# A message-passing layer on one core: SyncE fetches the rows of every 68th quad instead of every 48th, one batch in two steps instead of three in four

## The chip, the cores and the metric

The kernel runs on one core of one Trainium2 chip. The metric is device time in microseconds (us) of one launch. A core has five engines that run their own instruction streams: TensorE (PE, matrix multiply; PEld is its weight load), VectorE (DVE), ScalarE (ACT), GpSimd (POOL) and SyncE (SP, which here only issues DMA transfers). They meet through semaphores. 16 DMA engines move the data.

## What is computed

One equivariant graph layer over N = 12,500 nodes (160 features: 64 scalars and 32 vectors of 3) and E = 400,000 edges, sorted by destination, followed by a residual sum and a layer norm:

```python
h_s = s @ lin1_ws * a / 8                          # node features, 64 wide
h_v = einsum('nci,cd->ndi', v, lin1_wv) * a / sqrt(32)
hid = silu(edge_scalars @ fc_w1 / 8)               # per edge, 64 wide
w1, w2, w3, w4, w5 = split(hid @ fc_w2 / 8, ...)   # per edge, 224 wide
es, ev = h_s[edge_src], h_v[edge_src]              # gather of 160 floats per edge
m_s1 = w1 * es * e0;   m_s2 = w4 * (ev . e1) / sqrt(3)
m_v1 = (w2 * es) x e1; m_v2 = w3 * ev * e0; m_v3 = w5 * cross(ev, e1) / sqrt(2)
agg  = segment_sum(concat(...), edge_dst) / 4
o    = agg @ lin2;     pre = s @ sc + o
out  = layernorm(x + [silu(pre_s[:64]), sigmoid(pre_s[64:]) * pre_v])
```

The line that matters here is the gather: for each of 400,000 edges, one row of 160 floats (640 bytes) is read from a table that the kernel has written to HBM.

## The kernel before

**Start.** The first 61 us compute `h` for all nodes and write it to the table `h_tab` in HBM (L235 to L364). Constants and weights are loaded and scaled.

**Tiles, quads, steps.** The edges make 3,125 tiles of 128. Four tiles are a *quad* (`Q = 4`), and the main loop (L900) does one quad in a step: 782 steps. Six steps are a *chunk* of 24 tiles (`CT`).

**One step n, by engine.** The program is in the order in which it is written (`manual_schedule`, L891); nothing moves instructions afterwards.
- SP: `fetch(n + 4)` (L904). Where step n + 4 begins a chunk, it issues the load of that chunk's edge scalars, `es`, two transfers of 384 KB (L206). This load waits for the weights matmul of the step before (`mark`, L207), so SP can't run a chunk ahead. Now and then it also loads indices (L156), edge attributes (L157), and pieces for other work (L646, L692, L779, L781).
- SP: `fetch_rows(n)` (L905), which the change touches; see below.
- POOL: `gather` (L906, L473): four indirect DMAs, one for each tile, fetch 128 rows of `h_tab` each into `hg`. There are four `hg` buffers (the pool `deep`), so POOL can be four quads ahead of VectorE.
- PE: `weights` (L515), two matmuls for the 224 weights of each edge, from `hid`.
- ACT: copies out of PSUM and the silu (L460, L606, L608, L819), held back until the weights matmul of the step.
- DVE: `one_hot` (L578), `products` of weights and gathered rows (L525, L533), `select_quad` (L587), and additions into the accumulator (L631).
- PE: `add_tile` (L594) for the quad of two steps ago: a matmul with the one-hot rows sums the messages by destination.
- PE: `hide(n + 3)` (L939, L456), every second step, the hidden layer of two later steps. It reads `es`: this is where PE needs SP's load.
- PE and ACT now and then: transposes (L603), the second linear map (L623), and the end of finished nodes (L656 to L692).

**SyncE's own quads.** The step numbers in `own` (L478) are quads that POOL does not gather; SP fetches their rows one at a time. Before, `OWN = 48` gives 56, 104, ..., 776: 16 quads. For such a quad m:
- at step m - 54, `places` (L482) loads its 512 indices into `at_bytes`, four small transfers (L488);
- at step m - 46, DVE multiplies them by the 640 bytes of a row (L756), and `rows_of` (L491) makes 32 *jobs*;
- a job (L496) loads 16 indices into SP's registers (`BATCH = 16`, L497, a TENSOR_LOAD) and issues 16 transfers of 640 bytes, one for each row (L502; each is a register MOVE and a DMA);
- L759 says in which steps one job is issued: `n % EVERY and rows_due` with `EVERY = 4`, so in three steps of every four, 48 rows in four steps. The 32 jobs of quad m go out in steps m - 46 to m - 5;
- one `hq` buffer takes the rows (L493). Step m uses it in place of `hg` (L906).

What sets SP's order is thus written out by hand: a job stands in SP's queue ahead of the next step's `es` load.

Of the kernel before, what the change touches and what calls it, by code (L numbers as in the profile page):

```python
# [35 lines left out]
CT = 2 * SIDE  # L36
AHEAD = 3 * CT
NF = 4
OWN = 48
BATCH = 16  # L40
EVERY = 4

MARGIN = 128
NO = 16
# [13 lines left out]
def gnn_kernel(  # L58
# [176 lines left out]
    with tc.tile_pool(name="nodes", bufs=len(starts)) as nodes, tc.tile_pool(  # L235
# [84 lines left out]
        for c0, cn, quarters, cq, xa, xz in loaded:  # L320
# [6 lines left out]
            for t0 in range(0, nt, U):  # L327
                ps = nps.tile([P, U, P], F32, name="hp")
                for t in range(t0, min(t0 + U, nt)):
                    n = min(P, cn - t * P)  # L330
# [6 lines left out]
                if t0 + k < nt <= t0 + U:  # L337
                    n = cn - full * P
# [6 lines left out]
            for u in range(-(-cq // P)):  # L345
                n = min(P, cq - u * P)
# [10 lines left out]
            if cn > full * P:  # L357
                n = cn - full * P
# [118 lines left out]

    own = [n for n in range(OWN + 8, len(steps) - 4, OWN) if len(steps[n][2]) == Q]  # L478
    by_bytes = h_tab.rearrange("n d -> (n d)").bitcast(U8)
    row_bytes = 4 * D  # L480

    def places(pool, n):  # L482

        at_bytes = pool.tile([Q, P], I32, name="at_bytes")
        for k, (t, _, _) in enumerate(steps[n][2]):
            g, u = divmod(t, GT)
            with nc.allow_non_contiguous_dma(reason="the indices of one tile"):
                nc.sync.dma_start(at_bytes[k:k + 1], src[g][:, u:u + 1].rearrange("p u -> u p"))  # L488
        return at_bytes

    def rows_of(pool, at_bytes):  # L491

        hq = pool.tile([P, Q, D], F32, name="hq", bufs=1)  # L493
        flat_hq = hq.rearrange("p t d -> p (t d)").bitcast(U8)

        def job(t, p0):  # L496
            _, values = nc.values_load_multi_w_load_instructions(  # L497
                at_bytes[t:t + 1, p0:p0 + BATCH], engines=[ENG.SP], min_val=0,
                max_val=(N - 1) * row_bytes,
                skip_runtime_bounds_check_because="every entry of src is the index of a node")  # L500
            for p, v in enumerate(values, p0):
                nc.sync.dma_start(flat_hq[p:p + 1, t * row_bytes:(t + 1) * row_bytes],  # L502
                                  by_bytes[ds(v, row_bytes)][None])

        return hq, [lambda t=t, p0=p0: job(t, p0) for t in range(Q) for p0 in range(0, P, BATCH)]
# [198 lines left out]
    with tc.tile_pool(  # L704
# [43 lines left out]
        at_of, hq_of, rows_due = {}, {}, []  # L748

        def fetch_rows(n):  # L750

            for m in own:
                if n == max(1, m - OWN - 6):
                    at_of[m] = places(mine, m)
                if n == m - OWN + 2:
                    nc.vector.tensor_scalar_mul(at_of[m], at_of[m], float(row_bytes))  # L756
                    hq_of[m], jobs = rows_of(mine, at_of[m])
                    rows_due.extend((m, job) for job in jobs)
            if n % EVERY and rows_due:  # L759
                rows_due.pop(0)[1]()  # L760
            assert all(m > n for m, _ in rows_due)

# [128 lines left out]
        with tc.manual_schedule(engines={ENG.PE, ENG.DVE, ENG.Activation, ENG.Pool, ENG.SP}):  # L891
# [8 lines left out]
            for n, (c, i, tiles) in enumerate(steps):  # L900
                if 2 <= n < 2 + ZP // 2:
                    for k in range(2):
                        clear(2 * (n - 2) + k)
                fetch(n + 4)  # L904
                fetch_rows(n)  # L905
                hg = hq_of.pop(n) if n in own else gather(deep, [index(t) for t, _, _ in tiles])  # L906
                pw, marks[0] = weights(pw_ps, hids[c, i // 2], [(half, u - i // 2 * 4) for _, half, u in tiles])
# [39 lines left out]
            n = len(steps)  # L947
# [141 lines left out]
```

## Time and profile before

| | before |
|---|---|
| median of 3 runs | 6075.9 us (6064.73 to 6079.05) |
| the profiled execution, its own time | 6075.9 us |
| its span, first to last instruction | 6074.1 us |
| mean granted TensorE clock | 0.822 of full speed |
| PE busy / DVE / ACT / POOL | 4037.2 / 2446.3 / 853.9 / 2915.8 us |
| gathers by POOL (L473) | 3061, 948 ns mean each |
| rows by SP (L502) | 8192, in 512 jobs |
| HBM | 67 GB/s over the span |

How to read it. SP does no arithmetic: its instructions are sequencer instructions, which the profile does not count as busy, so SP has no share in the table of engines and has to be read from its own timeline and waits. In a timeline row the columns are the start, the length, the engine (`SPq` is SP's sequencer), the line, the operation, output and input, the number of instructions merged into the row, and in brackets the idle time before it and what ended it. A row of waits has the engine and line that waited, what it waited for, the total in us, the number of times, and the longest. "remote" is a semaphore whose sender the profile does not name. A row of a table by windows has the window, its length, and then busy us and instruction count of PE, PEld, DVE, ACT and POOL, the granted clock, the DMA engines' busy share and GB/s.

### The profile page before, as it was taken

The numbers are of one execution on the slowest core, as the hardware profiler recorded it, in microseconds if no ns is written. First come the engines' busy times: TensorE is split into PE (matmuls) and PEld (weight loads), VectorE is DVE, ScalarE is ACT, GpSimd is POOL, SyncE is SP. The second block draws the span as 40 slices with busy tenths as digits, with TensorE's granted clock in tenths as the row PEclk, the third lists the DMA queues.
The fourth block names the chain that finished last, engine by engine and source line by source line (L and its number), as shares of the span: only waits on it lengthen the run. The fifth ranks groups of instructions, "written<-read, shape, count | busy, mean of one in ns | idle before, by whom it ended". The sixth has DMA issues, their size and how long they took to land. (4 is left out here: it accounts for less than half of the span.)

```text
span 6074.1 us, 63034 instructions
## 1 busy us (share of the span) xinstructions
PE 4037.2 (66%) x14291; PEld 1740.4 (29%) x14291; DVE 2446.3 (40%) x6524; ACT 853.9 (14%) x2488; POOL 2915.8 (48%) x3080
## 2 busy tenths in 40 slices
PE   6667676676666666676767667667666666766666
PEld 3223222232322222232223223223222232322223
DVE  4434343343443433443434434344344343443434
ACT  2111111111111111111111111111111111111111
POOL 4444454444444444454545445445444444554443
PEclk8778788788888888788878788888788887888888
DMA  6223222222222222232222222223232222222222
GB/s 169 61 60 71 64 68 68 62 67 62 70 66 64 67 62 63 66 72 62 69 66 66 68 65 68 60 65 71 64 71 64 63 64 70 68 64 63 69 63 53
DMA packets 250347, 412.82 MB, mean 68 GB/s; under 512 B 88267, under 2 KB 180935, under 8 KB 249063
## 3 DMA queue, kind: packets, MB, share of 16 engines
q0 software_dynamic: 149200, 261.29, 18.0%
q1 hardware_dynamic: 100246, 147.32, 10.5%
q14 instruction: 273, 2.24, 0.1%
q8 instruction: 114, 1.87, 0.1%
q10 hardware_dynamic: 514, 0.10, 0.0%
HBM read 392.44 MB, written 16.00 MB: 67 GB/s over the span
## 5 line engine op out<-in xcount | busy, mean ns | idle before, releaser
L473 POOL DMA_INDIRECT hg<-h_tab,idx x3061 | 2901.5, 948 | 3072.2 <-DVE pr L533 1713.6
L515 PE MATMUL pw<-w,hid 128*128 128x448 f32 x3126 | 1544.4, 623 | 14.1 <-issue 9.1
L594 PE MATMUL pa<-pr,sel 128*64 128x416 f32 x6250 | 1339.0, 548 | 223.5 <-ACT sa L819 214.3
L578 DVE TENSOR_TENSOR pw<-rel,iota 128x64 f32<-128x64 int16 x782 | 181.8, 232 | 3195.3 <-PE pw L515 1424.6
L456 PE MATMUL misc<-es,w 128*128 128x512 f32 (+1 forms) x784 | 528.8, 763 | 944.2 <-DMA es<-in_es_t_dram 774.3
L533 DVE TENSOR_TENSOR pr<-pw,hg 128x384 f32<-128x384 f32 x2298 | 1128.5, 546 | 0.0
L515 PEld LDWEIGHTS pw<-w,hid 128*128 128x128 f32 x3126 | 671.6, 224 | 679.4 <-issue 653.3
L594 PEld LDWEIGHTS pa<-pr,sel 128*64 128x64 f32 x6250 | 393.9, 142 | 1167.4 <-issue 907.1
L606 ACT COPY tt<-misc 128x192 f32<-128x192 f32 x521 | 166.7, 320 | 3521.5 <-PE pw L515 1978.8
L603 PE MATMUL misc<-ident,sa 128*128 128x128 f32 x2084 | 387.1, 315 | 373.1 <-ACT tt L608 201.8
L525 DVE TENSOR_TENSOR pr<-pw,hg 128x512 f32<-128x512 f32 x766 | 528.9, 690 | 29.2 <-issue 1.6
L603 PEld LDWEIGHTS misc<-ident,sa 128*128 128x128 f32 x2084 | 255.0, 157 | 707.3 <-issue 364.8
L456 PEld LDWEIGHTS misc<-es,w 128*128 128x128 f32 x784 | 140.2, 224 | 1060.4 <-issue 981.6
L623 PE MATMUL misc<-tt,l 128*96 128x256 f32 (+5 forms) x1496 | 354.1, 385 | 1.7 <-ACT tt L608 1.5
L460 ACT ACTIVATE hid<-misc 128x512 f32<-128x512 f32 x392 | 238.4, 608 | 669.7 <-remote 397.6
L587 DVE TENSOR_TENSOR sel<-pw,eas 128x256 f32<-128x256 f32 x782 | 321.5, 411 | 0.3
L819 ACT COPY sa<-pa 128x416 f32<-128x416 f32 x521 | 267.9, 514 | 205.7 <-PE pw L515 123.4
L623 PEld LDWEIGHTS misc<-tt,l 128*96 128x96 f32 (+1 forms) x1496 | 226.5, 165 | 132.3 <-issue 57.1
L631 DVE TENSOR_TENSOR acc<-acc,os 96x32 f32 x1042 | 204.9, 197 | 25.1 <-ACT os L626 6.9
L785 PE MATMUL misc<-xs,scs 64*96 64x500 f32 x50 | 42.2, 939 | 234.9 <-DMA xs<-in_xs_t_dram 234.9
L656 PE MATMUL misc<-ident,acc 96*128 96x96 f32 x196 | 41.0, 297 | 200.9 <-DVE acc L631 166.0
L786 DVE TENSOR_TENSOR acc<-acc,misc 96x500 f32<-96x500 f32 x50 | 33.5, 670 | 261.3 <-PE misc L785 206.2
(87 smaller groups left out, 715.4 us busy)
## 6 DMA issues: line engine op xcount, KB each, us to landing
hq<-h_tab SPq DMA_DIRECT2D x8192, 0.6 KB
es<-in_es_t_dram SPq DMA_DIRECT2D x258, 384.0 KB
hg<-h_tab,idx POOLq DMA_INDIRECT x3061
h_tab<-ht POOLq DMA_DIRECT2D x6, 1280.0 KB
xt<-in_x_dram SPq DMA_DIRECT2D x23, 320.0 KB
out_dram<-y SPq DMA_DIRECT2D x23, 320.0 KB
xv<-in_xv_t_dram SPq DMA_DIRECT2D x25, 187.5 KB
xs<-in_xs_t_dram SPq DMA_DIRECT2D x25, 125.0 KB
```

The costliest lines, as they stand in the source:

```text
L456: nc.tensor.matmul(ph[:k, c], w1[:k, :k], es[:k, t0 * P + c0 * P:t0 * P + c1 * P], start=True, stop=True)
L460: return nc.scalar.activation(hid[:k, c], ph[:k, c], AF.Silu, scale=1.0 / math.sqrt(64))
L473: nc.gpsimd.indirect_dma_start(out=hg[:, t, :], out_offset=None, in_=h_tab, in_offset=bass.IndirectOffsetOnAxis(ap=i, axis=0))
L515: last = nc.tensor.matmul(pw[:, t:t + m, :NWT], hid[:m * S, c * P:(c + 1) * P], w2[:m * S, :m], start=True, stop=True)
L525: nc.vector.tensor_mul(two, pw[:, :n, :2 * S].rearrange("p t (k c) -> p t k c", k=2), hg[:, :n, None, :S].to_broadcast([P, n, 2, S]))
L533: nc.vector.tensor_mul(pr[:, :n, first:first + V3].rearrange("p t (i c) -> p t i c", i=3), pw[:, :n, None, 2 * S + k * V:2 * S + (k + 1) * ...
L587: nc.vector.tensor_mul(sel[:, :n], oh[:, :, None, :].to_broadcast([P, n, 4, W]), by_slot(tiles[0][0])[:, u:u + n, :, None].to_broadcast([P ...
L594: return nc.tensor.matmul(pa[half * ROWS:(half + 1) * ROWS, :NPR], sel[:, t].rearrange("p k w -> p (k w)"), pr, start=start, stop=stop)
L603: nc.tensor.transpose(pt[:, four * P:four * P + k], sa[:k, c:c + P], ident[:k, :k])
L623: nc.tensor.matmul(po[:, k, :nb], l2[r, terms[to, part, four]], a[:, :nb], start=(n == 0), stop=(n == len(of) - 1))
L631: nc.vector.tensor_add(window, window, os[:, :, b])
L819: closed.append(lambda: nc.scalar.copy(sa, pa[:, :NPR]))
```

## The change

The whole diff:

```diff
-OWN = 48
+OWN = 68
 BATCH = 16
-EVERY = 4
+EVERY = 2
...
-            if n % EVERY and rows_due:
+            if n % EVERY == 0 and rows_due:
                 rows_due.pop(0)[1]()
```

`own` becomes 76, 144, ..., 756: 11 quads instead of 16. The condition on L759 is turned round: a job is issued in the steps that `EVERY` divides, every second step, so 32 rows in four steps instead of 48. The jobs of quad m go out in steps m - 66 to m - 4, and its indices are loaded in step m - 74. The five quads that SP no longer fetches are gathered by POOL. In the program that is built, SP issues 5632 rows in 352 jobs and POOL 3081 gathers; PE and ACT have the same instructions as before, and DVE has five multiplications of `at_bytes` fewer. The first job is in step 10 in both kernels; the last is in step 752 instead of 771.

## The prediction

> **What bounds the kernel now.** I read the table of engines first, then the groups, the waits, and last SP's own timeline, because no engine of the table is full.
>
> ```profile
> PE 4037.2 (66%) x14291; PEld 1740.4 (29%) x14291; DVE 2446.3 (40%) x6524; ACT 853.9 (14%) x2488; POOL 2915.8 (48%) x3080
> ...
> hq<-h_tab SPq DMA_DIRECT2D x8192, 0.6 KB
> ```
>
> 782 steps in 6074.1 us are 7.8 us each. PE is busy two thirds of that. POOL issues a gather every 1.25 us when nothing stops it (0.95 us and 0.30 us before the next), 5.0 us for a quad, and so has more than a third of its time over. What stops them stands in the waits:
>
> ```profile
> POOL hg L473 <- DVE pr L533: 1713.6, 305, 18.9
> DVE pw L578 <- PE pw L515: 1424.6, 375, 24.8
> DVE pw L578 <- remote: 1377.1, 198, 13.3
> ...
> PE misc L456 <- DMA es<-in_es_t_dram: 774.3, 79, 22.3
> PE misc L785 <- DMA xs<-in_xs_t_dram: 234.9, 17, 19.1
> ```
>
> Followed from the top: POOL waits for VectorE to free an `hg` buffer, VectorE waits for PE's weights, and PE waits, at 79 of 130 chunks, for the load of `es`. Except for "remote", that is one chain, and it begins at a transfer that SP issues. SP's timeline says why the load is late:
>
> ```profile
> 2760.80 47.52 SPq L502 DMA_DIRECT2D hq<-h_tab  x80
> ...
> 2808.94 1.12 SPq L206 DMA_DIRECT2D es<-in_es_t_dram  x2
> ...
> 2813.48 48.49 SPq L502 DMA_DIRECT2D hq<-h_tab  x64
> 2862.07 1.13 SPq L206 DMA_DIRECT2D es<-in_es_t_dram  x2
> 2864.76 43.38 SPq L502 DMA_DIRECT2D hq<-h_tab  x80
> ```
>
> From one `es` load to the next (six steps, 47 to 53 us) SP does almost nothing but issue rows, without a pause. Its longest waits by line and releaser are 125.7 us (the first job of a quad, for VectorE), 81.7 and 75.2 us in total; over 6074 us it is full. The load stands in its queue behind the rows. So **SP's issuing sets the time**, and the other engines work in bursts behind it.
>
> **What a row costs.** Two stretches of the same timeline show that it depends on POOL:
>
> ```profile
> 3056.29 11.86 SPq L502 DMA_DIRECT2D hq<-h_tab  x32
> ...
> 3092.56 39.34 SPq L502 DMA_DIRECT2D hq<-h_tab  x48
> ```
>
> In the first POOL stands still (from 3048.6 to 3065.3 it waits for a buffer): 11.86 / 32 = 0.371 us a row, the job's register load included. In the second it gathers nearly all the time: 39.34 / 48 = 0.82 us. Why gathers slow SP the trace does not say; that they do is enough. I put it as a price of a gather:
>
> ```profile
> 2758.11:2808.94 50.83, 36.93 (x146) 16.40 (x142) 25.93 (x74) 9.51 (x23) 24.62 (x27) 0.94 0.27 61
> 2808.94:2862.07 53.13, 28.43 (x94) 11.45 (x94) 17.09 (x44) 5.82 (x21) 27.06 (x29) 0.76 0.29 69
> 2862.07:2908.83 46.76, 31.40 (x116) 13.98 (x116) 17.01 (x44) 5.53 (x16) 22.87 (x25) 0.83 0.25 60
> ```
>
> These three chunks last 150.7 us, with 224 rows (80, 64, 80) and 27 + 29 + 25 = 81 gathers (the last count of busy time in a row). The rows at 0.371 are 83.1 us; the other 67.6 us are 0.83 us a gather, SP's other loads included.
>
> **The change, part by part.**
> - *Rows removed.* 8192 - 5632 = 2560 rows with their 160 register loads leave SP's queue. At the quiet price that is 2560 x 0.371 = 950 us. I take the quiet price because the slow stretches belong to the gathers, whose number hardly changes: while they last SP gets few rows through, and a row that is taken away shortens the quiet part. The ends: 2560 x 0.82 = 2100 us if every removed row had stood beside gathers, and 0 if SP was not the bound after all.
> - *Gathers added.* Five quads, 20 gathers. POOL's own time is 20 x 1.25 = 25 us, hidden in the 1713.6 us that it waits for buffers; if that cover went, 25 us are the price. On SP's queue they cost 20 x 0.83 = +17 us.
> - *Index loads.* 20 loads of `at_bytes` fewer; four take 2.48 us of SP's queue in the trace, so -12 us. Five small VectorE multiplications fewer: nothing, VectorE is idle 60%.
> - *Spacing.* A job every second step puts 48 rows into a chunk where there were 72 (64 or 80 as SP reached them). By the two prices a chunk of 24 gathers asks of SP 48 x 0.371 + 24 x 0.83 = 37.7 us, 6.3 us a step. That is still above POOL's 5.0 us, so SP remains the bound, with less distance to the next.
> - *The end of a quad's rows.* The last job is issued four steps before the quad is used, five before. PE's wait at `es` keeps SP's lag to about two steps, so I price this at nothing; if the rows came late at each of the 11 quads by a step, 11 x 6.3 = 70 us would come back.
> - *No wait is added.* What is late next is the weights' release that VectorE sees as "remote" (1377.1 us) and POOL's pace.
>
> The sum: 6074 - 950 + 17 - 12 = 5129. The profiled execution's own time is 6075.9, 2 us above its span, and equal to the median, so **5130 us**. A second way, 130 chunks x 37.7 = 4900 and 78 us ahead of the first step and 32 behind the last, gives 5010 without any wait of SP, so the first sum holds about 120 us of them. Against PE's side: its waits for SP's loads are 774.3 + 234.9 = 1009 us, so a gain of 945 asks for nearly all of them to go, and hardly allows more by this path alone.
>
> *A rule against it.* The Trainium skill ("DMA: Bandwidth & Descriptors", section "Issuing engines are not separate DMA queues") says that starting DMAs from several engines saves only the time of the sequencer, "which is usually small relative to the DMA itself". By that, SP's queue is no bound and the sum would be POOL's alone, 6076 + 25 = 6101. The rows above disagree for transfers of 640 bytes: SP's queue is the full one.
>
> *A second.* The skill's "Perfetto Trace Analysis", section "DMA Optimizations", advises spreading DMAs over the engines that can issue them where generating descriptors is the bottleneck; this change takes work off SP and gives some to POOL. By the rows, SP is the one that is over its share.
>
> **The rivals.**
> 1. *SP stops being the bound.* For it: between 3062.68 and 3091.38, mostly without rows, VectorE starts six steps at 4.8 us each. If about half of the rows' slow price goes too and steps fall to 5.0 to 5.8 us, 782 of them and 110 us of ends are 4020 to 4650. Against it: 37.7 us a chunk are still asked of SP, and "remote" waits would lengthen the steps. Time about 4500. Chance 0.15.
> 2. *Part of the gain is eaten.* A release of the weights that comes late for another reason ("remote") takes the place of `es` at part of the chunks. For it: 1377.1 us, as much as the chain from `es`. If half of the rows' price is off the path, 6076 - 475 + 17 - 12 = 5606. Chance 0.12.
> 3. *Slower: gathers set the pace.* The lengths of the chunks follow the gathers (53 us with 29, 47 with 25), and rows only fill the time. Then 20 more gathers at 1.25 us are +25 us: 6101. It decides if PE's wait at `es` stays as it is with a third fewer rows. Against it: POOL idles 1713.6 us for buffers, and SP pauses for nobody. Chance 0.05; no measurable change, the two cancelling, 0.03.
> 4. *The change does not do what it says.* Counted in the built program, 5632 rows and 3081 gathers; no chance is left for it.
>
> **How the numbers follow.** The forecast, 5130, has a chance of 0.65, and by the two prices reaches from 4750 to 5400. Rival 1 has 0.15, rival 2 0.12, the rest 0.08. A range that leaves out 0.2 drops rival 3, the middle and most of rival 1: 4700 to 5620. Faster by over 0.3% (about what a measurement of this kernel can tell from no change) are the forecast and rivals 1 and 2, 0.92; within it 0.03; slower 0.05.
>
> **What would show it.** Right: 5632 rows and 3081 gathers; PE's wait at L456 for `es` far below 774 us, the one at L785 too; 38 to 40 us from one `es` load to the next, still filled with rows; POOL's wait for VectorE smaller; its gathers at 1.25 us as before. Rival 1: pauses in SP's timeline, steps near 5 us, POOL gathering without a stop. Rival 2: SP with pauses, L456 short, "remote" longer than 1377 us. Rival 3: L456 unchanged at about 774 us. The prediction is wrong if a row's price on SP goes up when the rows are spread: at 0.5 us instead of 0.371, the remaining 5632 would cost 730 us more and leave hardly any gain.

## The result, and the profile after

| | before | after |
|---|---|---|
| median | 6072.23 us (6064.73 to 6079.05, 4 runs) | 5375.94 us (5366.41 to 5391.65, 4 runs) |
| ratio | 1 | 0.8856 (95% interval 0.8831 to 0.8881) |
| profiled execution's own time, and its span | 6075.9, 6074.1 us | 5391.65, 5389.7 us |
| rows by SP, gathers by POOL | 8192, 3061 | 5632, 3081 |

The change is faster by 11.4%, about 695 us. The forecast was 5130 us, 945 us faster: the direction and the range hold, and a quarter of the expected gain did not come. The experiments ran at four other times, at which the kernel before took 5977, 5947, 6058 and, at the last, 4350 us, so each of them is told by its ratio to runs of the kernel before at the same time on the same chip.

The table of engines and the list of issues, of the changed kernel:

```profile
PE 3988.3 (74%) x14291; PEld 1735.6 (32%) x14291; DVE 2446.0 (45%) x6519; ACT 852.3 (16%) x2488; POOL 2934.7 (54%) x3100
...
hq<-h_tab SPq DMA_DIRECT2D x5632, 0.6 KB
```

Every engine did nearly the same work in less time. The waits (who waited for whom, total us, times, longest):

```profile
DVE pw L578 <- remote: 1615.3, 225, 15.2
POOL hg L473 <- DVE pr L533: 1344.6, 293, 14.0
...
DVE pw L578 <- PE pw L515: 878.8, 350, 14.1
...
PE misc L456 <- DMA es<-in_es_t_dram: 44.2, 10, 12.5
...
PE misc L785 <- DMA xs<-in_xs_t_dram: 33.0, 6, 7.3
```

PE's wait for `es` fell from 774.3 to 44.2 us and the one for `xs` from 234.9 to 33.0: the two loads that stood behind rows are in time. VectorE's wait for PE's weights fell by 546 us. But "remote" grew by 238 us and now is the first line. SP's timeline:

```profile
2734.22 1.12 SPq L206 DMA_DIRECT2D es<-in_es_t_dram  x2
...
2740.74 39.03 SPq L502 DMA_DIRECT2D hq<-h_tab  x48
2780.99 0.98 SPq L206 DMA_DIRECT2D es<-in_es_t_dram  x2
2784.83 23.63 SPq L502 DMA_DIRECT2D hq<-h_tab  x48
...
2812.09 1.92 SPq L206 DMA_DIRECT2D es<-in_es_t_dram  x2
2815.60 29.00 SPq L502 DMA_DIRECT2D hq<-h_tab  x48
2845.30 0.01 SPq L646 DMA_DIRECT2D xt<-in_x_dram  x1
2856.77 1.13 SPq L206 DMA_DIRECT2D es<-in_es_t_dram  x2
```

There are 48 rows between two `es` loads, as the text said, but SP is no longer full: from 2845.3 to 2856.8 it does nothing. Over the whole trace, its pauses of more than 2 us add up to 420 us before and 926 us after. Before, the chunks with 64 or 80 rows, 96 of 129, had almost none (under 0.1 us each on average). SP's list of waits says for what it pauses now:

```profile
SPq L206 <- PE pw L515: 287.2, 39, 38.2
```

It had 26.4 us of this wait before. The queue that everything stood behind now waits, part of the time, for PE. These three chunks have 31, 18 and 28 gathers by the table of windows:

```profile
2734.22:2780.99 46.77, 32.47 (x121) 13.15 (x122) 21.83 (x60) 7.65 (x26) 28.89 (x31) 0.85 0.32 76
2780.99:2812.09 31.10, 25.38 (x93) 11.49 (x93) 12.16 (x30) 3.69 (x11) 16.36 (x18) 0.89 0.36 81
2812.09:2856.77 44.68, 29.85 (x108) 11.84 (x108) 19.15 (x50) 5.39 (x16) 26.28 (x28) 0.89 0.35 80
```

They last 122.6 us, 40.9 each. Without the pause of 11.5 us SP used 37.0 us a chunk; they have 25.7 gathers each, for which the forecast's prices give 39.1. Over all 110 chunks with 48 rows, which have 24.0 gathers on average, the mean is 40.9 us, of which SP pauses for 4.0 and uses 36.9, near the forecast's 37.7. So the prices of a row and of a gather were right in their sum; that SP would stay the bound was not.

What "remote" is, VectorE's and POOL's timelines of the changed kernel show together. VectorE:

```profile
2112.74 0.23 DVE L578 TENSOR_TENSOR pw<-rel,iota 128x64 f32<-128x64 int16 x1 [11.92 <-remote]
```

The instruction waits for PE's weights, by the program and by the semaphore that it names. PE's four weights matmuls of that step lie between 2099.70 and 2101.37 in its timeline; VectorE was released 11.4 us later, and ScalarE's copy (L606) starts at the same 2112.74. POOL in that time:

```profile
2108.72 0.95 POOL L473 DMA_INDIRECT hg<-h_tab,idx  x1 [0.30 <-issue]
2115.36 0.94 POOL L473 DMA_INDIRECT hg<-h_tab,idx  x1 [5.69 <-DVE pr L533]
```

POOL had gathered since 2089.93, one every 1.25 us, ended at 2109.7, and three microseconds later the release came. The same can be counted over all steps of the changed kernel. A run of gathers ends where POOL pauses for over 0.5 us, and a release is late by the time from the end of PE's weights, or from when VectorE is free if that is later. Where the weights end in the first 4 us of a run, 24 of 261 releases are late by over 1 us; where they end after 8 us of it, 149 of 206 are, by 7.3 us on average. Other definitions shift these counts, but not the contrast.

### The profile page after: what moved, and what is told of

Read it like the earlier page. It is cut to its first block, busy times and chain, and to the rows that moved or that the text cites. A ratio compares the mean times of both kernels' runs of the same rounds, so it can differ in the third digit from the quotient of the medians.

```text
span 5389.7 us, 57721 instructions
## 1 busy us (share of the span) xinstructions
PE 3988.3 (74%) x14291; PEld 1735.6 (32%) x14291; DVE 2446.0 (45%) x6519; ACT 852.3 (16%) x2488; POOL 2934.7 (54%) x3100
## 3 DMA queue, kind: packets, MB, share of 16 engines
q1 hardware_dynamic: 92246, 145.66, 11.5%
## 5 line engine op out<-in xcount | busy, mean ns | idle before, releaser
L515 PE MATMUL pw<-w,hid 128*128 128x448 f32 x3126 | 1493.4, 605 | 16.8 <-issue 10.2
L515 PEld LDWEIGHTS pw<-w,hid 128*128 128x128 f32 x3126 | 650.7, 217 | 647.1 <-issue 617.7
L456 PE MATMUL misc<-es,w 128*128 128x512 f32 (+1 forms) x784 | 494.8, 718 | 264.3 <-ACT tt L608 92.2
L606 ACT COPY tt<-misc 128x192 f32<-128x192 f32 x521 | 166.8, 320 | 2595.9 <-remote 1233.0
L623 PE MATMUL misc<-tt,l 128*96 128x256 f32 (+5 forms) x1496 | 400.2, 421 | 55.7 <-ACT tt L608 40.6
L623 PEld LDWEIGHTS misc<-tt,l 128*96 128x96 f32 (+1 forms) x1496 | 250.8, 182 | 210.5 <-issue 80.4
L456 PEld LDWEIGHTS misc<-es,w 128*128 128x128 f32 x784 | 136.7, 218 | 367.1 <-issue 191.0
L656 PEld LDWEIGHTS misc<-ident,acc 96*128 96x128 f32 x196 | 22.4, 160 | 346.9 <-issue 212.4
L626 ACT COPY os<-misc 96x512 f32<-96x512 f32 (+2 forms) x68 | 38.4, 564 | 521.5 <-remote 169.8
```

Source lines behind the costliest of these rows:

```text
L456: nc.tensor.matmul(ph[:k, c], w1[:k, :k], es[:k, t0 * P + c0 * P:t0 * P + c1 * P], start=True, stop=True)
L515: last = nc.tensor.matmul(pw[:, t:t + m, :NWT], hid[:m * S, c * P:(c + 1) * P], w2[:m * S, :m], start=True, stop=True)
L623: nc.tensor.matmul(po[:, k, :nb], l2[r, terms[to, part, four]], a[:, :nb], start=(n == 0), stop=(n == len(of) - 1))
```

## The experiments

**No rows at all.** Is SP's issuing still what sets the time?

```diff
-    own = [n for n in range(OWN + 8, len(steps) - 4, OWN) if len(steps[n][2]) == Q]
+    own = []
```

> The changed kernel with no quad of SyncE's own: SP fetches no row, POOL gathers all 3125 tiles. Theory A (the forecast's: SP's issuing is still what sets the time, 0.37 us a row): 5632 rows fewer, so the time falls until POOL's pace of 5.0 us a step stops it, 4000 to 4600 us. Theory B (after the change PE's late releases set the time, they belong to the gathers, and a chunk's length follows its gathers at about 1.2 us each): 44 gathers more are +50 us, 5400 to 5450 us, with the waits called remote as long as before or longer (1615 us in the changed kernel). Theory C (the releases come late because rows and gathers meet): remote falls to about half, 4700 to 5000 us.

Measured: 5108.91 us, ratio 0.8542 (0.8522 to 0.8562). Its waits:

```profile
DVE pw L578 <- remote: 1476.5, 223, 13.5
ACT tt L606 <- remote: 1238.1, 151, 15.7
POOL hg L473 <- DVE pr L533: 1069.0, 282, 7.0
```

Theory A falls: 5632 rows fewer bring only 3.1% of the kernel before's time, 190 us, 0.034 us a row. Theory B has the mechanism ("remote" stays, SP is idle) but said slower by 50 us; the rows still cost something. Theory C, that rows and gathers must meet, falls too. Without one row, a chunk takes (5109 - 110) / 130 = 38.5 us, 6.4 us a step, at a time when the kernel before took 5977 us.

**The number of rows without the spacing.** The kernel before, with the first line of the change alone.

```diff
-OWN = 48
+OWN = 68
```

> One part of the change alone: 11 quads of SP's own as in the changed kernel, but a job in three steps of four as in the kernel before. Theory A (the number of rows counts): the same as the changed kernel, 5376 us within 1%. Rival (the spacing counts: while jobs go out three in four, the es loads are late again, and 43 of 68 steps run at 7.6 us as in the kernel before, the other 25 at 5.5 us): 68 steps are 464 us, 782 are 5340 plus 110, about 5450, with PE's wait at L456 for es at 400 to 500 us instead of nearly none. Slower than the changed kernel by 2% or more would say that the spacing did much of the work.

Measured: 5717.73 us, ratio 0.9557 (0.9522 to 0.9593). Its waits:

```profile
POOL hg L473 <- DVE pr L533: 1416.2, 289, 18.5
DVE pw L578 <- remote: 1403.3, 205, 13.2
...
PE misc L456 <- DMA es<-in_es_t_dram: 484.9, 59, 19.0
```

The rival holds, and more strongly than it said. The same 5632 rows, at the density of before, leave 485 us of the wait for `es`. SP's pauses of over 2 us add up to 1769 us here, nearly twice those of the changed kernel, and yet the time is longer: it matters where the rows stand, and not only how many they are. Of the change's 11.4%, the number of rows gives 4.4% and then the spacing 7.0%; the other order was not run.

**`es` on another queue.** In the kernel before, the loads leave SP's queue and all rows stay.

```diff
-    def load_chunk(c, queue=nc.sync, mark=None):
+    def load_chunk(c, queue=nc.scalar, mark=None):
```

> The kernel before, all 8192 rows and three jobs in four steps, but the two es loads of a chunk are issued from ScalarE's queue, so that they do not stand behind rows. If the place of es behind the rows is what costs the time: PE's wait at L456 goes (774 us before) and the time falls to 5400 to 5550 us, with no row removed. If SP's capacity is what costs it: SP lags now without a check, the rows of its own quads come late, and VectorE or POOL waits for hq; the time stays above 5850 us.

Measured: 6935.52 us, ratio 1.158 (1.1546 to 1.1615). Its waits:

```profile
POOL hg L473 <- DMA idx<-in_src_dram: 1063.9, 34, 63.3
...
PE misc L785 <- DMA xs<-in_xs_t_dram: 705.4, 21, 65.9
...
DVE y L669 <- DMA xt<-in_x_dram: 482.9, 16, 51.8
```

PE's wait for `es` is gone, all but 14 us, and the time rises. The other loads in SP's queue now come late, up to 66 us, and VectorE waits 291.5 us for the rows. That fits the expectation for SP's capacity, but it is not a clean test of it: SP's rows also waited 811.9 us in all for these `es` transfers, 75.2 us before, and SP's pauses add up to 1803 us. That the wait for `es` had held the program back to SP's pace, and that without it SP falls further behind, is argued and not shown.

**No gathers.** A constant tile takes the place of the gathered rows.

```diff
     def gather(pool, idx):
+        if still:
+            return still[0]
         hg = pool.tile([P, Q, D], F32, name="hg")
...
```

> The changed kernel without POOL's gathers: a constant tile stands in for the gathered rows (that part of the computation is left out); SP's rows and everything else stay. Theory B and C (late releases come from gathers): remote all but vanishes from 1615 us, a row costs 0.32 to 0.37 us throughout, and the steps fall to PE's own 4 to 5 us: 3300 to 4000 us. Theory A': rows alone make PE's releases late: remote stays above 1000 us and the time above 4600 us.

Measured: 3721.82 us in one run. The table of engines and the first waits:

```profile
PE 3529.2 (95%) x14291; PEld 1557.2 (42%) x14291; DVE 2434.3 (65%) x6520; ACT 862.2 (23%) x2488; POOL 14.1 (0%) x19
```

```profile
ACT tt L610 <- PE pw L519: 1639.8, 509, 7.9
DVE pw L582 <- PE pw L519: 1163.6, 750, 5.9
```

"remote" is gone with all 5632 rows still issued, and PE is the bound at 95%. The late releases need gathers and not rows. A row takes SP 0.40 us here on average over the whole run, from one issue to the next; in the changed kernel it is 0.84 us beside gathers and 0.42 elsewhere.

**Half the gathers, and half the bytes of each.** Both without rows by SP, from four fixed `hg` tiles. One gathers two tiles of a quad, the other all four with 320 bytes of each row.

```diff
...
+            idx = idx[:2]
...
```

> No rows by SP, and POOL gathers only two of the four tiles of a quad (the other two keep a constant: half of the gather is left out). Theory B (the gathers make the releases late, and the steps follow): 1563 gathers, 2.5 us of POOL in a step, no burst of 8 us; remote under 200 us and the time near the 3722 us without gathers, 3700 to 4000 us. Rival (the wait called remote belongs to the rest of the program as soon as POOL issues anything): above 4500 us.

```diff
-                out=hg[:, t, :], out_offset=None, in_=h_tab,
+                out=hg[:, t, :D // 2], out_offset=None, in_=h_tab.rearrange("n (k d) -> (n k) d", k=2),
...
```

> No rows by SP; as many gathers as in the kernel without rows (3125), each of 128 rows of 320 bytes instead of 640 (half of the gather is left out). If the number of gathered rows makes the releases late: 5000 to 5200 us, remote 1300 to 1600 us as without rows. If the bytes do: under 4400 us with remote under 500 us.

Measured, one run each: 3734.33 us with half the gathers, 5173.19 us with half the bytes, where the kernel before took 6058 us at that time. The waits with half the bytes, then with half the gathers:

```profile
DVE pw L584 <- remote: 1557.4, 229, 13.4
ACT tt L612 <- remote: 1316.2, 152, 15.9
```

```profile
POOL hg L480 <- DVE pr L540: 1719.4, 699, 8.2
ACT tt L613 <- PE pw L522: 1569.6, 482, 9.3
DVE pw L585 <- PE pw L522: 1114.0, 705, 6.2
```

5173 / 6058 = 0.854, the ratio of the kernel without rows: halving the bytes changes nothing. Half the gathers take the whole effect away. So it is the number of gathers, or of the rows that they fetch, in a stretch of time, and the effect sets in somewhere between 2 and 4 gathers a step. The Trainium skill ("Perfetto Trace Analysis", section "What "DMA-bound" means") says that for a kernel bound on DMA engines or on the sequencer that issues to them, large descriptors are what matter. The two runs agree in that fewer gathers helped and smaller ones did not; that the DMA engines are the bound here no run shows, as they were busy 0.32 to 0.36 of the time in the three chunks above.

**Fewer and more buffers.** If an unbroken run of gathers makes the releases late, `hg` buffers set how long it can be.

```diff
-        name="deep", bufs=4
+        name="deep", bufs=2
```

> The changed kernel with two hg buffers instead of four, so that POOL can gather at most two quads (8 gathers, 10 us) without a pause. In the profiles PE's release of the weights comes late almost only when POOL has gathered for 8 us or more without a pause. Theory B1 (a long burst of gathers makes the releases late): remote falls from 1615 to under 900 us and the time to 4700 to 5200 us. Rival (four buffers hide the gathers' landing; with two, VectorE waits for rows): the time rises to 5600 us or more, and VectorE waits for hg at L525.

Three more have no rows by SP (`own = []`) and two, three and six buffers:

> No rows by SP, two hg buffers. Theory B1: remote falls from 1476 to under 700 us, steps of 5.3 to 5.8 us, 4250 to 4700 us. Rival (buffers hide the landing): 5300 us or more. Theory B2 (lateness belongs to each gather, wherever it stands): no change within 2% of the 5109 us with four buffers.

> No rows by SP, three hg buffers: bursts of up to 12 gathers, 15 us. Theory B1: between two and four buffers, 4700 to 5000 us. Rival: between 5109 us and the time with two buffers on the other side, 5150 to 5300 us. Theory B2: 5109 us within 2%.

> No rows by SP, six hg buffers: bursts of up to 24 gathers, 30 us. Theory B1: longer bursts, more late releases, 5200 to 5500 us and remote above 1476 us. Rival (more buffers hide more): below 5050 us. Theory B2: 5109 us within 2%.

Measured, as ratios to the kernel before: 0.8884 (0.8837 to 0.8932) with rows and two buffers; without rows 0.8511 (0.8476 to 0.8545) with two, 0.8541 (0.8507 to 0.8575) with three, 0.8989 (0.8954 to 0.9023) with six, beside 0.8542 with four. The wait called remote without rows, with six buffers and then with two:

```profile
DVE pw L578 <- remote: 1839.5, 203, 24.3
```

```profile
DVE pw L578 <- remote: 1255.3, 213, 9.1
```

Six buffers do what Theory B1 said; two and three do not, as with two the wait falls only from 1477 to 1255 us, where under 700 was expected. The reason is in POOL's timeline: with two buffers it still makes runs of 12 to 20 gathers, 146 of its 357 runs, because VectorE frees a buffer before POOL has ended with the other. The number of buffers bounds a run only where VectorE stands still. The version without rows and with two buffers, 5060.67 us where the kernel before took 5947.2 us, is faster than both kernels of the change.

**Under half the rows, twice as far apart.**

```diff
-OWN = 68
+OWN = 136
...
-EVERY = 2
+EVERY = 4
```

> Five quads of SP's own (every 136th), a job in every fourth step: 2560 rows at half the changed kernel's density. If rows below SP's limit cost little each (0.034 us, from the changed kernel to none): ratio to the kernel before 0.869, between the changed kernel's 0.886 and the 0.854 without rows. If a row costs nothing while es is never late: 0.858 or less. If the forecast's 0.37 us a row held: 3072 rows fewer than the changed kernel are 1140 us, ratio 0.70.

Measured: 5307.66 us, ratio 0.8761 (0.8742 to 0.8781). PE waits 12.8 us for `es`. Its ratio lies between those of the changed kernel and of the one without rows, a little above the straight line (0.869): below SP's limit a row still costs, some 0.02 to 0.05 us, and the forecast's 0.37 is far off there.

**A pause after each quad**, without rows by SP, to keep the gathers from running on.

```diff
...
+        nc.gpsimd.iota(pad, pattern=[[1, 270]], base=0, channel_multiplier=0)
         return hg
```

> No rows by SP, four hg buffers; after the four gathers of a quad GpSimd counts through 270 numbers of one partition (about 1 us, from the 3.9 us of 1040 in the first microseconds of the trace), so a quad takes it about 6.2 us instead of 5.0. Theory B3 (gathers get through at some 1.6 us each whatever POOL does, 5109 us less 110 over 3125; what POOL issues faster only makes PE's releases late): the time stays within 1.5% of the kernel without rows, ratio 0.845 to 0.867, and remote falls from 1476 us to under 700. Theory B1 (an unbroken run of gathers is what makes them late): the pause breaks the runs, ratio below 0.835. Rival (POOL's own time is the bound): 782 pauses of 1.2 us are +940 us, ratio above 0.95.

Measured: 4184.72 us, and the kernel before 4350.19 us in 7 runs at that time; ratio 0.9621 (0.9605 to 0.9637). This run cannot decide between the three theories, because the kernel before itself took 27% less time than in the first experiments, on a chip of the same number. The profile with the pause has no large wait called remote, and POOL never waits long for a buffer:

```profile
ACT tt L608 <- PE pw L517: 1960.2, 508, 11.4
PEld pa L596 <- issue: 853.4, 2304, 1.3
POOL hg L474 <- issue: 817.8, 2951, 0.3
```

A quad takes POOL 5.23 us (from 2001.54 to 2006.77: four gathers and the pause, which is 0.34 us long and not the 1 us that was meant). 782 of them make 4090 of the 4182 us of the span: here POOL's own issuing is the bound. The 4350 us of the kernel before say that its time depends on something besides the kernel, which changed between these times. That it was the late releases which were absent from the kernel before at that time is not shown, as there is no profile of it; nor can it be told whether the pause had a part in their absence here.

## Why the prediction was right, and where it fell short

- **What bounds the kernel: right.** SP's queue of rows made `es` late. The change took 730 of 774 us from that wait, and the rows at their old density brought it back up to 485 us. That SP "is full" over 6074 us was too strong: it paused for 420 us, 7%, mostly in chunks with 48 rows or fewer.
- **Rows removed, 950 us: the term that was mis-sized.** On SP's queue the rows were worth that much and more: SP's time outside its pauses fell by 1190 us in the two profiles. But its pauses grew by 506 us, and the span fell by 684. With the two other small terms the rows measured 695 us in the medians. It is also not one price: removing 2560 rows at the old density gave 4.4%, about 270 us (0.105 us a row); spreading the rest gave 7.0%, about 425 us; removing the remaining 5632 would give 190 us (0.034 us a row). No run shows a row at its full price of 0.37 us in the time of the whole kernel.
- **Spacing, "SP remains the bound": the step that failed.** SP's need was priced well, 37.7 us a chunk against 36.9 measured. But the text set it against POOL's 5.0 us a step alone, 30 us a chunk. With no row at all the rest of the program needs 0.8542 x 6072 = 5187 us, 39.1 us a chunk, so SP was no longer the bound, and the forecast of 5130 us was below what the program takes without rows. That is 57 of the 246 us that are missing. The other 189 are what the remaining rows still cost: the changed kernel takes (5376 - 110) / 130 = 40.5 us a chunk. That they cost it because SP's queue and the rest of the program each need about 38 us, unevenly, is argued; the numbers are measured.
- **PE's side, "hardly allows more": half of the account.** The two waits for SP's loads fell by 932 us, nearly the whole 945. VectorE's wait called remote rose by 238 us. The difference, 694 us, is close to the gain, but no run shows that these waits add up like this.
- **Rival 2 named what takes the place of `es`**, the releases called remote: 1377 to 1615 us. It priced them at 475 us; 250 were lost. The changed kernel shows all of its signs: pauses in SP's timeline, a short wait at L456 and a longer "remote". The forecast's own sign, chunks still filled with rows, did not come. That 5376 us lies within the forecast's 4750 to 5400, at its edge, is owed to the size of the loss and not to the mechanism.
- **Rival 1 took six steps after a stall, 4.8 us each, for the pace of the program.** They were run on buffers that POOL had filled ahead, as it stood waiting for a buffer up to 3065.3. Without any rows, steps take 6.4 us, and not 5.0 to 5.8.
- **Rival 3, gathers set the pace, +25 us: wrong in its time, half right in its reason.** The lengths of the chunks do follow the gathers, in both kernels; but PE's wait for `es`, which was to stay, fell, and before the change SP was over its limit as well.
- **The end of a quad's rows, at nothing: right.** POOL's wait for `hq` fell from 389.1 to 65.0 us.
- **The Trainium skill's rule** that issuing DMAs costs a sequencer little ("DMA: Bandwidth & Descriptors", "Issuing engines are not separate DMA queues") would have given 6101 us. With one DMA for each 640 bytes the measurement, 5376 us, is on the other side.

**Open.** Why PE's release comes late when gathers run on for 8 us, what resource they share, and what made the kernel before 27% faster at one time. VectorE and ScalarE are released at the same moment in the step shown, which points to PE's signal and not to one receiver; but the profile models where a matmul ends, so that the matmuls themselves end late is not ruled out. Whether a gather lands late in the same time was not measured: VectorE did not wait for `hg` there, but these rows had been fetched ahead. What the change is worth where the kernel before takes 4350 us was not tried.

## What to carry to other kernels

An engine that only issues transfers has no busy share in the table of engines: read its timeline from one urgent load to the next, and see whether it ever pauses. The price of an issue removed counts only down to the point where the next limit takes over, so before multiplying it, find the pace of the program with that queue empty; here one kernel with no rows would have given it. Where a fixed number of small transfers must share a queue with loads that someone waits for, spreading them evenly was worth more than removing a third of them (7.0% against 4.4%, the removal first).

## What the runs showed of the hardware

- Gathers of 128 rows, issued every 1.25 us without a pause, go with slower work elsewhere: an SP row takes 0.84 us beside them and 0.42 apart from them (0.40 in the run without gathers), and PE's releases after 8 us of such a run are late in 149 of 206 steps, by 7.3 us on average. Two gathers a step show next to none of the late releases, four do show them, at 320 bytes a row as at 640, at a time when the kernel before took 6058 us; at the time of the 4350 us four gathers a step, with a short pause after each four, showed none.
- The same kernel took 4350 us in all 7 runs at one time and 5947 to 6072 us at the others; on the chip numbered 6 it did both (5977 and 4350). A ratio taken at one time is safe; times taken at different times are not to be set side by side.
- Without gathers PE ran at a granted clock of 0.992 with 95% busy, before the change at 0.822 with 66%.
